# Scan outputs on TensorE: 64 output rows and 128 columns in two column groups instead of 32 rows and 64 columns in four

## The chip, the cores and the metric

The kernel runs on one core of a Trainium2 chip. The metric is device time in microseconds of one execution, smaller is better. Engines are named as in the profile: PE (TensorE matmuls), PEld (its weight loads), DVE (VectorE), ACT (ScalarE), POOL (GpSimd), SP (the engine that issues all DMAs here).

## The reference: what is computed

Sixteen images of 256 channels and 32 x 32 = 1024 positions go through two layers, each added to its input: group norm and a transformer block with four heads (attention over 1024 positions, then a feed-forward part), then group norm and a selective state-space layer. The second layer holds the recurrence that fills most of the time:

```python
def step(h, inp):
    d_t, B_t, C_t, u_t = inp
    dA = jnp.exp(d_t[..., None] * A)
    h = dA * h + (d_t * u_t)[..., None] * B_t[:, None, :]
    y = jnp.einsum('bdn,bn->bd', h, C_t)
    return (h, y)
h0 = jnp.zeros((B, D_INNER, D_STATE), u.dtype)
_, ys = lax.scan(step, h0, (delta..., Bm..., Cm..., u...))
```

D_INNER is 512, D_STATE is 64, and the scan runs over 1024 time steps. So an image has 512 x 64 recurrences of 1024 steps, and for every channel and time step a sum over 64 states of h times C. Everything is float32.

## The kernel before

**Units.** The recurrences of an image (a batch, in the code) are cut into 256 units. A unit is two channels of 64 states each, on 128 partitions, and all 1024 steps. With 16 batches there are 4096 units. For unit n the kernel does:

- `load`: a DMA brings the row of delta u of the two channels, repeated over 64 partitions each, into a tile `dub` (L928, 512 KB).
- `inputs`: POOL multiplies the tile by B in place (L933). B of the batch is in the tile `bt`.
- `decay`: PE spreads delta over the partitions by two bf16 products into a PSUM tile `a` of 1024 columns (L942), and ACT takes the exponential in place (L944). The pool `aps` has two such tiles.
- `scan`: DVE runs the recurrence over 1024 steps (L950) and writes row i of a buffer `h` of eight units.

**Products by C.** When eight units are done, `outputs` sums over the states. PE sums over partitions, but C changes with every time step. So the tile `cd` holds, for each time step, the 64 values of C in a column of their own (two columns, one for each channel of a unit; `spread_c` fills it from the tile `ct`). A product takes 16 columns of `cd` that are not zero, those of 8 time steps, in a block of 32, and h of the 8 units at the same 8 time steps: 64 columns. Of the 32 x 64 results only those where both time steps agree are wanted. Two such products (c = 0 and 1) fill disjoint rows of the 32 and are added in PSUM. Four groups g go to PSUM partitions 0, 32, 64 and 96, so to four column groups of PE. A float32 product is two instructions (records) in the trace, so the 128 products of eight units are 256 records, in eight steps of 32 records, one at each of the next eight units. The sums `yb[:, :256]` are copied to `y2` by ACT (L981) after every second step, four times in eight units.

**The turn.** After that, products of `y2` by `turn`, pieces of the unit matrix (L987), pick the wanted results and put the time steps on partitions: 32 products, 64 records, in one burst for every eight units. The weights that PE loads for them are columns of `y2` that stand eight elements apart. ACT copies the result to `yo` (L991), and two DMAs write it out.

**What else runs.** While batch b is scanned, the attention layer and the inputs of batch b + 1 and the last part of batch b - 1 are worked off in small steps (Python generators that yield shares of time; `rate` spreads them over the 256 units). The last batch has only the closing part of the one before it beside it. The steps that matter below are the scores (`s_ps`, L449), the weights and values (`st_ps` L520, `av` L508), the projections and the gate (L657, L679, L707).

**Order.** The order of instructions on PE, ACT, DVE and POOL is as written: in each unit `load(n + 6)`, `inputs(n + 4)`, one step of `outputs`, `scan(n)`, `decay(n + 2)`, then side steps. `decay(n + 2)` writes the PSUM tile that `scan(n)` reads. SP's order is left to a scheduler. All waits are semaphores which the framework places.

Of the kernel before, what the change touches and what calls it, by code (L numbers as in the profile page):

```python
# [11 lines left out]
F32 = mybir.dt.float32  # L12
# [7 lines left out]
P = 128  # L20
C = 256
KC = C // P
L = 1024
# [27 lines left out]
def attention_then_scan_kernel(  # L51
# [18 lines left out]
    nc = tc.nc  # L70
    B = x.shape[0]

    def pool(name, bufs, **kw):
        return ctx.enter_context(tc.tile_pool(name=name, bufs=bufs, **kw))

    const = pool("const", 1)
# [2 lines left out]
    half = pool("half", 4)  # L79
    ptp = pool("ptp", 4)  # L80
    small = pool("small", 2)
    dutp = pool("dutp", 7)
    blk = pool("blk", 2)
    hst = pool("hst", 1)
    dram = pool("dram", 2, space=DRAM)
# [44 lines left out]
    def hs(h):  # L130
        return ts(h, HL)
# [15 lines left out]
    ident = const.tile([P, P], F32, name="ident")  # L147
# [21 lines left out]
    for k in range(ND):  # L169
# [4 lines left out]
        for j in range(2):  # L174
# [3 lines left out]
                start=(j == 0), stop=(j == 1),  # L178
# [3 lines left out]
    for e in range(2):  # L182
        some = ident[ds(64 * e, 48), ds(64 * e, 48)].rearrange("p (r j i) -> p r i j", r=3, j=2)
# [8 lines left out]
        nc.vector.tensor_reduce(par[:, j : j + 1], ident[:, j:P:2], AX.X, ALU.add)  # L192


    turn = const.tile([P, 8, 2, 8], F32, name="turn")
    grid = ident.rearrange("p (m x j) -> p x j m", x=8, j=2)
    for c in range(8):
        nc.vector.tensor_copy(turn[:, c], grid[:, c])


# [22 lines left out]
    yb = yps.tile([P, HL], F32, name="yb", tag="yb")  # L223
    nc.vector.memset(yb, 0.0)

    cd = hst.tile([P, L // 16, 64], F32, name="cd", tag="cd")
# [129 lines left out]
    def fetches(to, src, n=KC):  # L356
        return [partial(fetch, to, src, k) for k in range(n)]


    def first_norm(b, besides=()):  # L360
        xs, tok = [], []
        kept = state[b]["kept"] = dram.tile([C, L], F32, name="kept", tag="kept")
        if "x" in state[b]:
            xs = state[b].pop("x")
        else:
            for go in fetches(xs, x[b]):
                go()
            yield 0.4
        gn = [work("gn") for _ in range(KC)]
        yield from along(group_norm(xs, gn), fetches(tok, pos) + [None] * 3 + list(besides))  # L370
        for k in range(KC):
            nc.gpsimd.tensor_tensor(tok[k], tok[k], gn[k], ALU.add)
            nc.sync.dma_start(kept[ts(k, P), :], tok[k])
            yield 0.6
# [461 lines left out]
    def gate_loads(b):  # L836
        st = state[b]
        (wo_s,), bring = weights((w_o, ND))
        ys, us, zs, gs, xs = [], [], [], [], []
        come = [  # L840
            partial(fetch, to, st[name], d)
            for d in range(ND) for to, name in ((ys, "ys"), (us, "ud"), (zs, "zs"))
        ]
        come.insert(1, bring[0])
        come += [
            partial(fetch, to, st[name], k) for k in range(KC) for to, name in ((gs, "gs"), (xs, "xr"))
        ]
        st["gate"] = ys, us, zs, gs, xs, wo_s, come[4:]
        return come[:4]

    def gate_and_store(b):
# [51 lines left out]
    units = [  # L903
        (b, k, q, e, i)
        for b in range(B) for k in range(ND) for q in range(4) for e in range(2) for i in range(SLOTS)
    ]
    blocks, loaded, decays = {}, {}, {}
    now = {}

    def load(n):  # L910
        b, k, q, e, i = units[n]
        st = state[b]
        if (k, q, e, i) == (0, 0, 0, 0):
            bt = hst.tile([P, L], F32, name="bt", tag="bt")
            ct = hst.tile([P, L], F32, name="ct", tag="ct")
            for v, lo in ((bt, 0), (ct, NS)):
                src = st["rows"][lo : lo + NS, :]
                nc.sync.dma_start(v, src.unsqueeze(1).to_broadcast([NS, 2, L]))
            blocks[b] = {"bt": bt, "ct": ct}
        if i == 0:  # L920
            pieces = blk.tile([P, HL], BF16, name="pieces", tag="pieces")
            rows = ds(((k * 4 + q) * 2 + e) * 48, 48)
            for hf in range(2):
                nc.sync.dma_start(pieces[ds(64 * hf, 48)], st["dps"][rows, hs(hf)])
            blocks[b, k, q, e] = pieces
        du = dutp.tile([P, L], F32, name="dub", tag="dub")
        src = st["dus"][ts(k, P)].rearrange("(q j i e) c -> q e i j c", q=4, j=2, i=SLOTS)[q, e, i]
        nc.sync.dma_start(du, src.unsqueeze(0).to_broadcast([NS, 2, L]))  # L928
        loaded[n] = du

    def inputs(n):
        v = loaded[n]
        nc.gpsimd.tensor_tensor(v, v, blocks[units[n][0]]["bt"], ALU.mult)  # L933
# [20 lines left out]


    def spread_c(b, c):
        ct = blocks[b]["ct"].rearrange("p (a c x) -> p a c x", c=2, x=8)
        for j in range(2):
            nc.scalar.activation(
                cd[:, :, 48 * c + j : 48 * c + j + 15 : 2], ct[:, :, c],  # L960
                AF.Identity, scale=par[:, j : j + 1],
            )

# [2 lines left out]

    def outputs(b, k, q, e):
        hbuf = now["h", e]
        y2 = hst.tile([P, 4, 256], F32, name="y2", tag="y2")
        for r in range(4):  # L970
            for s in range(4):
                for c in range(2):
                    for g in range(4):
                        at = 256 * r + 64 * s + 16 * g + 8 * c
                        nc.tensor.matmul(  # L975
                            yb[ts(g, 32), ts(s, 64)],
                            cd[:, at // 16, ts(c, 32)], hbuf[:, :, at : at + 8],
                            start=(c == 0), stop=(c == 1),
                        )
                if s == 3:  # L980
                    nc.scalar.copy(y2[:, r], yb[:, :256])  # L981
                if s % 2 == 1:
                    yield
        some = yb[:, 256:384].rearrange("p (j m x) -> p x j m", j=2, m=8)
        for x in range(8):
            for r in range(4):
                nc.tensor.matmul(  # L987
                    some[ts(r, 32), x], y2[:, r, x:256:8], turn[:, x], start=True, stop=True
                )
        yo = blk.tile([P, P], F32, name="yo", tag="yo")  # L990
        nc.scalar.copy(yo, yb[:, 256:384])  # L991
        for _ in range(3):
            yield
        to = state[b]["ys"][ds(k * P + 32 * q, 32)].rearrange(
            "(j i e) (a c) -> e j a i c", j=2, e=2, a=16
        )
        for j in range(2):
            nc.sync.dma_start(to[e, j], yo[:, ts(j, 64)])

    def prepare(b):  # L1000
        return chain(first_norm(b), attention_layer(b), scan_inputs(b))
# [6 lines left out]
    def gap(share, rate):  # L1008
        return share if share < 1 else max(1.0, share / rate)

    def rate_for(shares, room):
        lo, hi = 0.01, 10.0
        for _ in range(40):
            mid = (lo + hi) / 2
            lo, hi = (mid, hi) if sum(gap(w, mid) for w in shares) > room else (lo, mid)
        return hi
# [10 lines left out]
    running = []  # L1027
    side, rate, due = iter(()), 1.0, 0.0
    for n, (b, k, q, e, i) in enumerate(units):
        at = n % UNITS  # L1030
        if at == 0:
            parts = [prepare(b + 1)] if b + 1 < B else []
            total = steps * len(parts)
            if b > 0:
                if b + 1 < B:
                    parts = [
                        first_norm(b + 1, gate_loads(b - 1)), gate_and_store(b - 1),
                        attention_layer(b + 1), scan_inputs(b + 1),
                    ]
                else:  # L1040
                    parts = [gate_and_store(b - 1)]
                total = total + GATE
            side = chain(*parts)
            rate, due = rate_for(total, UNITS - AHEAD - 3), 0.0
        if at == UNITS - AHEAD:
            for _ in side:
                pass
            if b + 2 < B:
                for go in fetches(state[b + 2].setdefault("x", []), x[b + 2]):
                    go()  # L1050
        if n + AHEAD < len(units):
            load(n + AHEAD)
        if n + LEAD < len(units):
            inputs(n + LEAD)
        if n % UNITS == SLOTS:
            spread_c(b, 1)
        if i == 0 and n > 0:
            running.insert(0, outputs(*units[n - 1][:4]))
        for g in list(running):
            if next(g, g) is g:  # L1060
                running.remove(g)
        if n % UNITS == SLOTS - 1:
            spread_c(b, 0)
        scan(n)
        if n + 2 < len(units):
            decay(n + 2)
        if at >= (1 if b + 1 < B else 8):
            due -= 1.0
            while due <= 0.0:
                due += gap(next(side, 1e9), rate)  # L1070
# [76 lines left out]
```

## Time and profile before

| what | value |
|---|---|
| median of 3 runs | 12746.27 us (12697.65 to 12832.91) |
| profiled execution, its own time | 12803.03 us |
| span of the profiled execution | 12801.3 us |
| PE busy, PEld busy | 9998.7 us (78%), 5523.7 us (43%) |
| DVE busy | 11287.1 us (88%) |
| POOL busy | 10025.9 us (78%) |
| ACT busy | 7502.7 us (59%) |
| mean granted TensorE clock | 0.792 |

The busy time of an engine is the union of its instructions. PE's instructions are pipelined, so its busy time is not its full use. The line `PEclk` gives the clock that PE was granted in each fortieth of the span, in tenths of full speed. A view by windows gives the same numbers for chosen stretches of time. The view of the chain follows the work that ended last back from the end, piece by piece; a piece such as `PE yb L975 x32` is the time that these 32 records added to it.

### The profile page before, as it was taken

How to read it: one execution, taken by the hardware profiler on the slowest of the kernel's cores; microseconds unless marked ns; L12 is line 12 of the kernel's file. 1: busy time of each engine (PE TensorE's matmuls, PEld its weight loads, DVE VectorE, ACT ScalarE, POOL GpSimd, SP SyncE). 2: the span in 40 equal slices, each digit the busy share in tenths (PEclk: the TensorE clock that was granted, in tenths of full speed). 3: DMA queues.
4: the chain of work that ended last, by engine and by line, in shares of the span. 5: the costliest groups of instructions: out<-in, count | busy, mean ns of one | idle time of the engine just before them, and what ended most of it. 6: DMA issues, size and time to landing. Idle time of an engine off the chain costs nothing.

```text
span 12801.3 us, 424578 instructions
## 1 busy us (share of the span) xinstructions
PE 9998.7 (78%) x186800; PEld 5523.7 (43%) x186800; DVE 11287.1 (88%) x7480; ACT 7502.7 (59%) x10726; POOL 10025.9 (78%) x4201
## 2 busy tenths in 40 slices
PE   7776878868788786986978868787786877868777
PEld 2344444444444444443444444444444444444444
DVE  2799998989989899798798989989998999989998
ACT  3565665656566565565565656565565655656554
POOL 0587878878788788687778878787787878878798
PEclk8887978879788787686778878798787988879756
DMA  1567666676666767466566676666767667676676
GB/s 54 185 225 246 214 223 239 213 246 217 223 237 218 239 221 244 163 216 231 180 224 236 218 245 217 228 232 219 237 222 241 217 214 237 222 244 213 230 251 229
DMA packets 1038404, 2820.12 MB, mean 220 GB/s; under 512 B 290370, under 2 KB 368451, under 8 KB 1036548
## 3 DMA queue, kind: packets, MB, share of 16 engines
q1 hardware_dynamic: 1036548, 2792.97, 64.1%
q8 instruction: 1459, 23.90, 0.7%
q14 instruction: 397, 3.25, 0.1%
HBM read 2513.82 MB, written 261.62 MB: 217 GB/s over the span
## 4 chain that ended last, share of the span: by engine, by line
PE 41%; DVE 30%; issue 12%; ACT 8%; DMA 6%; POOL 2%; SPq 1%; DVEq 0%; POOLq 0%; ACTq 0%
DVE h L950 23%; PE s_ps L449 8%; PE yb L975 8%; PE a L942 6%; ACT a L944 4%; DMA dub<-dus 3%; PE av L508 3%; PE st_ps L520 3%; POOL dub L933 2%; PE z_ps L657 2%; PE yb L987 2%; PE g_ps L707 2%; PE m_ps L887 1%; DVE u L693 1%; DMA xs<-ud 1%
## 5 line engine op out<-in xcount | busy, mean ns | idle before, releaser
L933 POOL TENSOR_TENSOR dub<-dub,bt 128x1024 f32<-128x1024 f32 x4096 | 9800.5, 2416 | 2644.6 <-DMA dub<-dus 2458.8
L950 DVE TENSOR_TENSOR_SCAN h<-a,dub 128x1024 f32<-128x1024 f32 x4096 | 9204.1, 2276 | 708.7 <-ACT a L944 401.3
L944 ACT ACTIVATE a<-a,acol 128x1024 f32<-128x1024 f32 x4096 | 4464.2, 1090 | 3086.7 <-PE a L942 2954.9
L975 PEld LDWEIGHTS yb<-h,cd 128*32 128x32 f32 x131072 | 2517.7, 129 | 2704.1 <-issue 1303.3
L942 PE MATMUL a<-pieces,pick 48*128 48x512 bf16 x8192 | 1922.7, 460 | 2204.2 <-DVE h L950 2088.4
L975 PE MATMUL yb<-h,cd 128*32 128x64 f32 x131072 | 3292.0, 253 | 336.3 <-ACT y L981 231.8
L942 PEld LDWEIGHTS <-pick 48*128 48x128 bf16 x8192 | 571.7, 95 | 2612.3 <-issue 2204.8
L981 ACT COPY y<-yb 128x256 f32<-128x256 f32 x2048 | 763.3, 373 | 753.0 <-PE yb L975 744.2
L449 PE MATMUL s_ps<-kd,q 32*64 32x512 f32 x2044 | 593.4, 669 | 18.0 <-DVE mx L428 9.0
L508 PE MATMUL av<-pt,vv 128*64 128x512 f32 x2048 | 602.0, 668 | 2.8 <-ACT sums L497 1.6
L528 ACT ACTIVATE pt<-st_ps 128x512 f32<-128x512 f32 x1024 | 552.7, 597 | 73.5 <-PE st_ps L520 72.7
L987 PE MATMUL yb<-turn,y 128*32 128x16 f32 x32768 | 591.1, 214 | 4.9 <-issue 3.8
L520 PE MATMUL st_ps<-sp 33*128 33x512 f32 x2048 | 581.3, 643 | 3.4 <-ACT pt L528 3.4
L987 PEld LDWEIGHTS yb<-turn,y 128*32 128x32 f32 x32768 | 573.2, 159 | 5.8 <-issue 4.3
L449 PE MATMUL s_ps<-k,q 32*64 32x512 f32 x2048 | 569.1, 645 | 0.0
L428 DVE CUSTOM_DVE_ANT_0 over<-s_ps,over 128x512 f32<-128x512 f32 x512 | 343.8, 673 | 207.9 <-issue 120.6
L991 ACT COPY yo<-yb 128x128 f32<-128x128 f32 x512 | 135.3, 264 | 601.0 <-PE yb L987 581.3
L707 PE MATMUL g_ps<-w,xp 128*128 128x256 f32 x1464 | 455.2, 450 | 0.0
L707 PEld LDWEIGHTS g_ps<-w,xp 128*128 128x128 f32 x1464 | 367.9, 326 | 66.7 <-issue 58.5
L454 ACT ACTIVATE over<-s_ps 128x512 f32<-128x512 f32 x511 | 303.5, 594 | 86.7 <-PE s_ps L449 86.7
L887 PE MATMUL m_ps<-w,xs 128*128 128x256 f32 x1024 | 319.5, 462 | 11.5 <-POOL xs L862 11.5
L693 DVE SCALAR_TENSOR_TENSOR u<-up,cwh,u 128x1024 f32<-128x1024 f32 x192 | 301.7, 1571 | 28.0 <-ACT u L685 27.7
(178 smaller groups left out, 7103.6 us busy)
## 6 DMA issues: line engine op xcount, KB each, us to landing
dub<-dus SPq DMA_DIRECT2D x4096, 512.0 KB
dps<-pc SPq DMA_DIRECT2D x384, 128.0 KB
pieces<-dps SPq DMA_DIRECT2D x1024, 48.0 KB
xs<-in_x_dram SPq DMA_DIRECT2D x64, 512.0 KB
xs<-kept SPq DMA_DIRECT2D x64, 512.0 KB
zs<-z SPq DMA_DIRECT2D x64, 512.0 KB
ud<-u SPq DMA_DIRECT2D x64, 512.0 KB
dus<-du SPq DMA_DIRECT2D x64, 512.0 KB
```

Source lines behind the costliest of these rows:

```text
L449: nc.tensor.matmul(s[ts(e, 64)], q4[r, ts(c, 64)], keys[r], start=True, stop=True)
L508: nc.tensor.matmul(av[ts(e, 2 * DH)], vv[j // (NJ // 2)][:, j % (NJ // 2), 2 * pair + e, :], pts[e], start=(j == 0), stop=(j == NJ - 1),)
L520: nc.tensor.matmul(s, ka[r, ts(j, P)], qa[r, hs(hf)], start=True, stop=True)
L528: nc.scalar.activation(pt, s, AF.Exp)
L707: nc.tensor.matmul(ps[:, ts(q, C)], xp[k][:, ds(first + t, P, 4)], wg_s[:, k, t, :], start=(k == 0 and t == 0), stop=False,)
L933: nc.gpsimd.tensor_tensor(v, v, blocks[units[n][0]]["bt"], ALU.mult)
L942: nc.tensor.matmul(a[:, hs(hf)], w, pieces[r], start=True, stop=True)
L944: nc.scalar.activation(a, a, AF.Exp, scale=acol[:, at : at + 1])
L950: nc.vector.tensor_tensor_scan(now["h", e][:, i, :], decays.pop(n), loaded.pop(n), 0.0, ALU.mult, ALU.add)
L975: nc.tensor.matmul(yb[ts(g, 32), ts(s, 64)], cd[:, at // 16, ts(c, 32)], hbuf[:, :, at : at + 8], start=(c == 0), stop=(c == 1),)
L981: nc.scalar.copy(y2[:, r], yb[:, :256])
L987: nc.tensor.matmul(some[ts(r, 32), x], y2[:, r, x:256:8], turn[:, x], start=True, stop=True)
```

## The change

A product now takes the 32 columns of `cd` of 16 time steps in a block of 64, and h of eight units at 16 time steps: 128 columns. Two groups g go to PSUM partitions 0 and 64. So eight units have 64 products (128 records) in eight steps of 16 records. Each step fills 256 columns of `yb`, and each step is followed by a copy to `y2`, which has 8 x 256 columns instead of 4 x 256: eight copies in eight units. The first step of a new group of eight units is put before the turn of the group before it, and its copy after it. The turn has 16 x 2 products, each with a weight block of 64 columns of `y2`, 16 elements apart, and 8 columns of `turn`. The tiles `bt` and `ct` are taken from the pool of `dub`, which has 8 buffers instead of 7, so that B and C of the next batch no longer have one fixed buffer each. In the order that the program is built in, the loads of delta u wait for the scan seven units back, as before, except for some of them around the start of a batch, which wait for the one six or five units back.

```diff
-    dutp = pool("dutp", 7)
+    dutp = pool("dutp", 8)
...
-    turn = const.tile([P, 8, 2, 8], F32, name="turn")
-    grid = ident.rearrange("p (m x j) -> p x j m", x=8, j=2)
-    for c in range(8):
+    turn = const.tile([P, 16, 2, 4], F32, name="turn")
+    grid = ident.rearrange("p (m x j) -> p x j m", x=16, j=2)
+    for c in range(16):
...
-            bt = hst.tile([P, L], F32, name="bt", tag="bt")
-            ct = hst.tile([P, L], F32, name="ct", tag="ct")
+            bt = dutp.tile([P, L], F32, name="bt", tag="dub")
+            ct = dutp.tile([P, L], F32, name="ct", tag="dub")
...
-        ct = blocks[b]["ct"].rearrange("p (a c x) -> p a c x", c=2, x=8)
+        ct = blocks[b]["ct"].rearrange("p (a c x) -> p a c x", c=2, x=16)
+        to = cd.rearrange("p (a c) w -> p a c w", c=2)
...
-                cd[:, :, 48 * c + j : 48 * c + j + 15 : 2], ct[:, :, c],
+                to[:, :, c, 32 * c + j : 32 * c + j + 31 : 2], ct[:, :, c],
...
-        y2 = hst.tile([P, 4, 256], F32, name="y2", tag="y2")
-        for r in range(4):
-            for s in range(4):
+        y2 = hst.tile([P, 8, 256], F32, name="y2", tag="y2")
+        for u in range(8):
+            for s in range(2):
                 for c in range(2):
-                    for g in range(4):
-                        at = 256 * r + 64 * s + 16 * g + 8 * c
+                    for g in range(2):
+                        at = 128 * u + 64 * s + 32 * g + 16 * c
                         nc.tensor.matmul(
-                            yb[ts(g, 32), ts(s, 64)],
-                            cd[:, at // 16, ts(c, 32)], hbuf[:, :, at : at + 8],
+                            yb[ts(g, 64), ts(s, 128)],
+                            cd[:, at // 16], hbuf[:, :, at : at + 16],
                             start=(c == 0), stop=(c == 1),
                         )
-                if s == 3:
-                    nc.scalar.copy(y2[:, r], yb[:, :256])
-                if s % 2 == 1:
-                    yield
-        some = yb[:, 256:384].rearrange("p (j m x) -> p x j m", j=2, m=8)
-        for x in range(8):
-            for r in range(4):
+            if u == 0:
+                yield
+            nc.scalar.copy(y2[:, u], yb[:, :256])
+            yield
+        some = yb[:, 256:384].rearrange("p (j m x) -> p x j m", j=2, m=4)
+        sums = y2.rearrange("p (h u) w -> p h (u w)", h=2)
+        for x in range(16):
+            for h in range(2):
                 nc.tensor.matmul(
-                    some[ts(r, 32), x], y2[:, r, x:256:8], turn[:, x], start=True, stop=True
+                    some[ts(h, 64), x], sums[:, h, x:1024:16], turn[:, x], start=True, stop=True
                 )
...
-        if i == 0 and n > 0:
-            running.insert(0, outputs(*units[n - 1][:4]))
-        for g in list(running):
+        fresh = [outputs(*units[n - 1][:4])] if i == 0 and n > 0 else []
+        for g in fresh:
+            next(g)
+        for g in running + fresh:
             if next(g, g) is g:
                 running.remove(g)
+        running += fresh
```

## The prediction

> **What bounds the kernel now.** I read the page first: shares, slices, chain, groups.
>
> ```profile
> span 12801.3 us, 424578 instructions
> PE 9998.7 (78%) x186800; PEld 5523.7 (43%) x186800; DVE 11287.1 (88%) x7480; ACT 7502.7 (59%) x10726; POOL 10025.9 (78%) x4201
> PEclk8887978879788787686778878798787988879756
> PE 41%; DVE 30%; issue 12%; ACT 8%; DMA 6%; POOL 2%; SPq 1%; DVEq 0%; POOLq 0%; ACTq 0%
> L950 DVE TENSOR_TENSOR_SCAN h<-a,dub 128x1024 f32<-128x1024 f32 x4096 | 9204.1, 2276 | 708.7 <-ACT a L944 401.3
> L975 PE MATMUL yb<-h,cd 128*32 128x64 f32 x131072 | 3292.0, 253 | 336.3 <-ACT y L981 231.8
> L987 PEld LDWEIGHTS yb<-turn,y 128*32 128x32 f32 x32768 | 573.2, 159 | 5.8 <-issue 4.3
> ```
>
> DVE is nearly full, yet PE holds more of the chain: the bound changes by stage. So I asked for windows over batch 9 (in order: score stage, values, light stage, gate), the score stage of batch 7 (second row), and batch 15 (last):
>
> ```profile
> 7665.30:7734.60 69.30, 69.30 (x1202) 28.44 (x1203) 67.40 (x73) 42.75 (x64) 56.57 (x25) 1.00 0.55 192
> 6062.40:6189.10 126.70, 126.70 (x1202) 43.98 (x1200) 69.92 (x73) 45.74 (x64) 56.19 (x24) 0.50 0.31 105
> 7758.90:7883.60 124.70, 112.72 (x2248) 53.42 (x2249) 107.41 (x50) 96.52 (x148) 110.52 (x48) 0.93 0.67 231
> 7902.30:8031.40 129.10, 91.04 (x1746) 51.04 (x1745) 120.20 (x80) 68.40 (x91) 100.48 (x42) 0.72 0.62 214
> 8031.40:8128.80 97.40, 89.01 (x1496) 57.13 (x1495) 94.70 (x58) 58.28 (x80) 88.34 (x32) 0.96 0.68 225
> 12348.00:12716.40 368.40, 271.32 (x6760) 185.16 (x6760) 359.30 (x170) 205.11 (x261) 368.40 (x161) 0.60 0.71 242
> ```
>
> Columns: length, busy time of PE, PEld, DVE, ACT, POOL, then granted clock. The score stage is all PE; the same 24 units take 69.3 us at clock 1.00 and 126.7 at 0.50 (batches 6 and 7 of this execution; the others are at 1.00). Values and gate are near PE's limit (90%, 91%), the light stage is DVE's (93%), batch 15 POOL's (100%). The chain in the two score stages gives a unit piece by piece:
>
> ```profile
> 7687.48 0.58 PE yb L975 x32
> 7690.84 0.96 PE yb L987 x64
> 6057.65 3.61 PE s_ps L449 x8
> 6061.26 1.01 PE yb L975 x32
> 6089.01 0.54 PE a L942 x2
> ```
>
> At half clock 3.61 + 1.01 + 0.54 + 0.96/8 = 5.28 us a unit; at full clock (scores 1.86, decay 0.32 in the same view) 1.86 + 0.58 + 0.32 + 0.12 = 2.88.
>
> [...] L508 (64 columns, two groups) [...] in the trace its two records start 7 ns apart. [...] Here 110, 132 and 188 ns for 32, 64 and 128 columns side by side (L975, L508, L679): 0.81 ns a column over a base of 83. For strided columns [...] the trace has 160 ns for 32 (L987) and 329 for 128 (L707). [...] The trace has only 0.5 and 1.0, changing on multiples of 3.41 us; but a PE busy for 126.7 of 126.7 us stays at 0.50, so busy time is not the measure. [...]
>
> **What sets the clock.** I weighted each record by rows x columns of the array in use (a score record 32 x 64, so 1/8; four product records at once, all), times its streaming time at full clock, and summed over each clock window. Of half-clock windows under 0.25, none of 924 was followed by a full one; 0.30 to 0.35, 25% of 162; over 0.40, all 221. Of full-clock windows under 0.20 none of 143 stayed full; 0.25 to 0.30, 24% of 99; 0.30 to 0.35, 90% of 250. So a window needs use of about 0.3.
>
> **The change part by part.**
>
> Products. In the trace four records of 64 columns start 7 ns apart, the next four 55.8 ns later at full clock, 106.7 at half: time goes with columns and clock, not with records. L508's pairs of 512 columns stand 8 such steps apart. Two records of 128 columns should take two steps, 109 or 213 ns. A unit has 8 rounds before and after, so 8 x 53.4 = +0.43 us at full clock (0.58 to 1.01), +0.85 at half (1.01 to 1.86). Bounds: -0.1 (cost per record, half as many) to +0.9.
>
> The turn. Its 16 rounds of four take 62 ns each at both clocks, so matmul streaming isn't the limit. I take it to be the strided weight load: 62/32 = 1.94 ns a column; L707, one group of 128 strided columns, is spaced 233 ns, 1.8 a column[...]. So groups load side by side and the depth counts: 64 columns cost 124 ns, with two groups there are 32 rounds, 3.97 us for 0.96. Bounds: if it is writing 16 scattered columns to PSUM, 8 columns halve it (1.0 us in all); if a round is a fixed 62 ns, 2.0. I take 3.97: the weight loads are 50 ns longer than contiguous ones.
>
> Clock. The burst uses almost no array (8 columns a record), so a window half inside it falls to about 0.2: the clock drops at each burst. In the score stage at half clock a unit of 6.51 us would hold, as streaming time at full clock times share of the array: products 8 x 0.107 x 1, decay 0.21 x 0.75, four score pairs 4 x 0.427 x 0.25; in all 1.44, a use of 0.22. A window that holds a whole product block reaches 0.33. So the full clock seldom returns. I take one third full, two thirds half.
>
> Stage by stage, for 15 batches with work beside the scan:
> - Scores, 32 units. Full clock 1.86 + 1.01 + 0.32 + 3.97/8 = 3.69; half 3.61 + 1.86 + 0.54 + 0.50 = 6.51; mixed 5.57. 13 batches x 32 x (5.57 - 2.88) = 1119, two x 32 x 0.29 = 19. Together +1138.
> - Values, 50 units at 124.7/50 = 2.49. From the chain, a pair of L520 is 0.43, of L508 0.50; 1.25 and 1.125 pairs a unit: 1.10 + 1.01 + 0.32 + 0.50 = 2.93. So 0.44 x 50 x 15 = 330, and clock dips, 1.5 us at six bursts: 135. Together +465.
> - Gate, 33 units at 2.95: 1.56 of its own matmuls + 1.83 = 3.39, +218.
> - Light stages, 16 bursts. The product itself hides behind DVE. Not the burst, since `decay(n + 2)` stands behind it on PE, and behind that the exponential and the scan. From the end of scan n - 1 at half clock: decay 0.54, side work 0.3, products 1.86, burst 3.97, then ACT's yo copy 0.26, y2 copy 0.37 (now ahead of the exponential), exponential 1.09, hand-overs 0.15: 8.5 us, 7.5 at full clock (before: 4.3). DVE has two scans and three units' side work meanwhile, 3 x 3.0 - 2.28 = 6.7, or 8.1 where a unit takes 3.45. Late by 0 to 1.8; at 1.0, 16 x 15 = +240.
> - Batch 15, 32 bursts, 2 to 3 us late, partly recovered behind POOL: +80.
> - ACT's four more copies of 0.37 us in eight units: 0.19 a unit beside 41% idle time, counted only above. If values became ACT's, up to 0.1 x 50 x 15 = 75.
> - B and C. At the start of batch 8 the timeline has DVE waiting 6.51 us for POOL, and POOL for the delta u behind B. B's load now waits for a scan five units earlier: up to 6.5 x 15 = 98 gained. Loads with one or two units less lead are some 14 a batch, and cost nothing while POOL keeps four units of lead.
>
> Sum: 1138 + 465 + 218 + 240 + 80 - 98 = +2043 on the profiled 12803, so 14850. The profiled execution is 57 us above the median; one score stage at half clock costs 32 x 2.40 = 77, so runs differ by such stages. The forecast isn't moved by it, as all score stages end mixed.
>
> **Rivals.**
> A. The burst takes 2 us or less (PSUM writing or a fixed round). Scores +0.56 a unit at full clock, 233; values 142; gate 94; batch 15 20; B -98: 13200, up to 13700 with some clock dips. For it: the turn's outputs are scattered. Against: the long weight loads.
> B. The burst as forecast, but the clock holds in the score stage: scores +337 in place of 1138, without the values' dips 13910. For it: between bursts the use at full clock would be 1.44/3.19 = 0.45. Against: the window rule.
> C. Faster: cost by record, not by column. Products then stay at 0.58 or less and the burst at 0.96. Larger array use ends the half-clock score stages (-154) and B saves 98: 12550. It decides once a round of two wide records takes under about 65 ns. Against: the spacing doubles exactly with the clock, and L508.
>
> **Numbers.** Forecast 0.43; A 0.25; B 0.20; C 0.06; no change within 1%, if hidden costs and gains cancel, 0.04; above the range 0.02. About 1% is what can be told from no change here. The range 13150 to 15400 holds the forecast, A and B, with scores wholly at half clock (+500) at the top. Faster 0.06, same 0.04, slower 0.90.
>
> **What would show it.** A product piece of 16 records at 1.01 or 1.86 us; the turn's 64 records near 4 us and its weight loads near 210 ns; score windows of 24 units near 130 us with a clock between 0.5 and 0.8; DVE waiting for the exponential once in eight units; no 6.5 us wait at a batch's start. A turn under 2.2 us makes A right, a score clock above 0.9 B, product rounds under 65 ns C.

## The result and the profile after

The changed kernel takes 15685.15 us (median of 4 runs, 15678.48 to 15745.78). The kernel before takes 12777.05 us (median of 4). The ratio is 1.2326, with a 95% interval of 1.2275 to 1.2376: 23% slower. The forecast was 14850, with a range up to 15400. The direction and the main mechanisms were right, the size was not.

The page of the changed kernel, the lines that answer to those shown of before (span, busy times, clock by slices, chain, groups):

```profile
span 15688.6 us, 295315 instructions
PE 14172.0 (90%) x121264; PEld 8858.3 (56%) x121264; DVE 11442.4 (73%) x7488; ACT 8229.2 (52%) x12774; POOL 9950.9 (63%) x4201
PEclk8687786877878777787777877778687786877888
PE 69%; DVE 14%; ACT 7%; issue 6%; DMA 3%; SPq 0%; POOL 0%; DVEq 0%; POOLq 0%; ACTq 0%
L950 DVE TENSOR_TENSOR_SCAN h<-a,dub 128x1024 f32<-128x1024 f32 x4096 | 9252.8, 2280 | 2114.8 <-ACT a L944 1592.8
L976 PE MATMUL yb<-h,cd 128*64 128x128 f32 x65536 | 5688.8, 329 | 371.0 <-ACT y L983 248.6
L989 PEld LDWEIGHTS yb<-turn,y 128*64 128x64 f32 x32768 | 1864.0, 203 | 1.4 <-ACT y L983 1.4
```

PE now holds 69% of the chain, for 41% before. It has a third fewer records and is busy 4173 us longer. Its records overlap in the trace: 65536 of 329 ns in the mean stand in the 5688.8 us of L976's line. DVE does the same work (busy 11442.4 us for 11287.1) in a longer span. Its wait for the exponential ahead of the scan, the first releaser in L950's line, grew from 401.3 to 1592.8 us.

The windows over the same units as in the prediction (batch 9: scores, values, light stage, gate; batch 15 last; columns length, then busy PE, PEld, DVE, ACT, POOL, then clock):

```profile
9311.10:9462.10 151.00, 151.00 (x818) 68.12 (x816) 69.86 (x73) 49.64 (x76) 59.54 (x26) 0.53 0.26 92
9491.80:9647.00 155.20, 150.31 (x1478) 90.95 (x1478) 108.39 (x49) 104.84 (x173) 113.42 (x49) 0.89 0.51 184
9671.60:9810.90 139.30, 122.46 (x1106) 80.02 (x1105) 121.41 (x81) 74.63 (x111) 99.53 (x42) 0.80 0.59 200
9810.90:9933.70 122.80, 118.59 (x984) 80.73 (x983) 100.83 (x57) 63.37 (x96) 80.15 (x32) 0.92 0.52 174
15172.10:15592.50 420.40, 358.92 (x4200) 276.37 (x4199) 360.98 (x169) 232.48 (x341) 372.52 (x161) 0.83 0.61 211
```

The score stage went from 69.3 to 151.0 us for its 24 units, and its clock from 1.00 to 0.53. PE is busy in all of it. The other stages lose less, and their clocks change less, except in batch 15. There the clock rises from 0.60 to 0.83, and in the light stage from 0.72 to 0.80.

The chain in that score stage gives a unit's pieces:

```profile
9404.59 3.61 PE s_ps L449 x8
9408.20 1.91 PE yb L976 x16
9410.11 0.54 PE a L942 x2
9416.16 3.41 PE yb L989 x60
```

3.61 + 1.91 + 0.54 + 3.4/8 = 6.48 us. From the starts of the scans the trace has, in the mean over the batches, 6.48 us for units 50 to 57 and 6.3 for units 58 to 73. The prediction had 6.51 for the half clock.

Over all batches, from the starts of the scans in each trace, by stage (15 batches; units 0 to 39, 136 to 175 and 208 to 255 light, 40 to 79 scores and what ends them, 80 to 135 values, 176 to 207 gate):

| stage | before | after | difference | forecast |
|---|---|---|---|---|
| scores | 1887 | 3189 | +1302 | +1138 |
| values | 2134 | 2703 | +569 | +465 |
| gate | 1519 | 1848 | +328 | +218 |
| light, with the batch starts | 6189 | 6785 | +596 | +142 |
| batch 15 | 607 | 691 | +85 | +80 |

### The profile page after: what moved, and what is told of

Its sections match the earlier page's. It is cut to its first block, busy times and chain, and to the rows that moved or that the text cites. A ratio compares the mean times of both kernels' runs of the same rounds, so it can differ in the third digit from the quotient of the medians.

```text
span 15688.6 us, 295315 instructions
## 1 busy us (share of the span) xinstructions
PE 14172.0 (90%) x121264; PEld 8858.3 (56%) x121264; DVE 11442.4 (73%) x7488; ACT 8229.2 (52%) x12774; POOL 9950.9 (63%) x4201
## 4 chain that ended last, share of the span: by engine, by line
PE 69%; DVE 14%; ACT 7%; issue 6%; DMA 3%; SPq 0%; POOL 0%; DVEq 0%; POOLq 0%; ACTq 0%
PE yb L976 22%; PE s_ps L449 10%; PE yb L989 10%; DVE h L950 10%; PE a L942 6%; PE av L508 4%; PE st_ps L520 3%; ACT a L944 3%; PE g_ps L707 2%; PE m_ps L887 2%; PE z_ps L657 2%; ACT y L983 2%; DMA dub<-dus 1%; PE u_ps L679 1%; DMA xs<-ud 1%
## 5 line engine op out<-in xcount | busy, mean ns | idle before, releaser
L950 DVE TENSOR_TENSOR_SCAN h<-a,dub 128x1024 f32<-128x1024 f32 x4096 | 9252.8, 2280 | 2114.8 <-ACT a L944 1592.8
L976 PEld LDWEIGHTS yb<-h,cd 128*64 128x64 f32 x65536 | 4561.8, 167 | 2883.6 <-ACT y L983 917.4
L976 PE MATMUL yb<-h,cd 128*64 128x128 f32 x65536 | 5688.8, 329 | 371.0 <-ACT y L983 248.6
L983 ACT COPY y<-yb 128x256 f32<-128x256 f32 x4096 | 1530.1, 374 | 3205.0 <-PE yb L976 3187.5
L989 PEld LDWEIGHTS yb<-turn,y 128*64 128x64 f32 x32768 | 1864.0, 203 | 1.4 <-ACT y L983 1.4
L989 PE MATMUL yb<-turn,y 128*64 128x8 f32 x32768 | 1848.4, 253 | 0.9 <-ACT y L983 0.9
L942 PEld LDWEIGHTS <-pick 48*128 48x128 bf16 x8192 | 479.0, 95 | 1734.7 <-issue 1681.5
L449 PE MATMUL s_ps<-kd,q 32*64 32x512 f32 x2044 | 869.4, 953 | 18.1 <-DVE kd L423 9.1
L449 PE MATMUL s_ps<-k,q 32*64 32x512 f32 x2048 | 848.9, 932 | 0.0
L508 PE MATMUL av<-pt,vv 128*64 128x512 f32 x2048 | 640.0, 707 | 2.9 <-ACT sums L497 1.6
L449 PEld LDWEIGHTS s_ps<-k,q 32*64 32x64 f32 x2048 | 208.7, 199 | 535.4 <-issue 504.8
```

What stands on the lines that cost most here:

```text
L449: nc.tensor.matmul(s[ts(e, 64)], q4[r, ts(c, 64)], keys[r], start=True, stop=True)
L508: nc.tensor.matmul(av[ts(e, 2 * DH)], vv[j // (NJ // 2)][:, j % (NJ // 2), 2 * pair + e, :], pts[e], start=(j == 0), stop=(j == NJ - 1),)
L942: nc.tensor.matmul(a[:, hs(hf)], w, pieces[r], start=True, stop=True)
L950: nc.vector.tensor_tensor_scan(now["h", e][:, i, :], decays.pop(n), loaded.pop(n), 0.0, ALU.mult, ALU.add)
L976: nc.tensor.matmul(yb[ts(g, 64), ts(s, 128)], cd[:, at // 16], hbuf[:, :, at : at + 16], start=(c == 0), stop=(c == 1),)
L983: nc.scalar.copy(y2[:, u], yb[:, :256])
```

## The experiments

**Parts of the change taken out (e1, e2, e3).** First the turn, then half of the products, then both. e1 in the changed kernel:

```diff
-        for x in range(16):
+        for x in range(1):
             for h in range(2):
```

> The changed kernel with 1 of the turn's 16 column steps kept, so 15/16 of the turn is left out; products unchanged. Theory 1 (the burst of 3.6 us drops the clock in the score stage and stands ahead of the decay elsewhere): score stage back to clock above 0.9 and near 3.2 us a unit (1.86 + 1.01 + 0.32), for 6.48; light stages nearly as in the kernel before; in all about 13100. Theory 2 (the light stages lose by the wider products, since side matmuls queue behind them): scores as in theory 1, but light stages keep most of their +600; about 13500. Rival (the clock falls because of the wider products, not because of the burst): the score stage stays at 0.5 and near 6.0 us a unit, 14400.

e2 in the changed kernel:

```diff
-                for c in range(2):
+                for c in range(1):
...
-                            start=(c == 0), stop=(c == 1),
+                            start=True, stop=True,
```

> The changed kernel without the products of c = 1: half of the products are left out, so that a unit has 8 records of 128 columns and products take 0.58 or 1.01 us as before; the turn is whole. Theory 1: scores stay at half clock, 3.61 + 1.01 + 0.54 + 0.45 = 5.6 us a unit; values and gate each get 0.43 us a unit back; light stages stay slow; about 14700. Theory 2: light stages lose most of their +600 as well, 14200. Rival (products set the clock): score stage at full clock, 3.2 us a unit, below 13500.

e3 has both edits.

> Both of the last two left out: half of the products and 15/16 of the turn. What remains of the change is the double number of copies, their place ahead of the exponential, and B and C from the other pool. All theories with PE as the cause: score stage 2.77 us a unit at full clock in all batches, in all 12500 (between 12350 and 12650). Rival (ACT's copies, or the loads with less lead, cost time by themselves): above 12800.

Measured: e1 13040.37, e2 15008.71, e3 12651.67 us (one run each; the kernel before took 12682.1 on that chip). The window rows of e1's and e2's score stage in batch 9, in this order, columns as above:

```profile
7753.10:7830.50 77.40, 77.40 (x638) 34.87 (x636) 69.67 (x73) 46.59 (x76) 56.41 (x25) 1.00 0.53 172
8911.60:9043.10 131.50, 131.50 (x626) 48.17 (x624) 69.81 (x75) 49.41 (x76) 60.49 (x26) 0.53 0.32 105
```

Without the burst the clock stays at 1.00 although the products are wide; with it the clock is 0.53 although the products are halved. So in this stage the burst decides the clock, and the rival of e1 and e2 falls. 77.4/24 = 3.2 us a unit is 1.86 + 1.01 + 0.32 of the expectation.

The three spans and the changed kernel's make a table of two by two: neither part 12650, wide products alone 13039 (+389), burst alone 15007 (+2357), both 15689 (+3039, which is 293 more than the sum). The burst is the main cost by a factor of six. The remaining parts (more copies, their place, B and C's pool) cost little: e3 is not above the kernel before, though it is just above the range expected for it. It also lacks the short turn that the kernel before has, so a small cost of these parts may be hidden by that.

In the light stages the same table reads: neither 6170, products 6325 (+155), burst 6540 (+370), both 6785 (+615). So theory 2, products as the main cause there, is wrong; theory 1, products quite hidden, is not exact either. e2 came out above both expectations: values 471 and light stages 351 above before, each more than I had for a burst beside narrow products.

**The burst alone, in the kernel before (e4).**

```diff
-        for x in range(8):
+        for x in [x for x in range(8) for _ in range(4)]:
             for r in range(4):
```

> The kernel before with each matmul of the turn issued four times (same result): a burst of about 3.84 us in place of 0.96, products unchanged. Theory 1: the clock falls to half in all score stages, 3.61 + 1.01 + 0.54 + 0.48 = 5.6 us a unit; light stages late by the burst; about 14500. Theory 2: the same scores, light stages little changed, 14100. Rival (a burst on its own does not drop the clock): score stage at 1.0 and 3.25 us a unit, below 13500.

Measured: 16473.84 us, above every expectation. The burst is not 3.84 us. Its median from first to last record is 6.83 us, since PE stands still in it without a wait that the profile shows:

```profile
L987 PE MATMUL yb<-turn,y 128*32 128x16 f32 x131072 | 2299.1, 217 | 1374.0 <-issue 1372.5
```

1372.5 us of idle time by "issue" in 512 bursts is 2.7 us a burst. The clock of the score stages was 0.57 to 0.69, for 0.94 to 1.00 in 13 of the 15 before, so this burst beside narrow products did lower it. For the sizes the run says nothing, since it was not the burst that was meant. What holds PE up in a run of 256 records was not tried.

**Why the burst takes its time (e5b).** The copies write `y2` in another order, so that each weight load reads 64 neighbours:

```diff
-        y2 = hst.tile([P, 8, 256], F32, name="y2", tag="y2")
+        y2 = hst.tile([P, 2, 16, 64], F32, name="y2", tag="y2")
...
-            nc.scalar.copy(y2[:, u], yb[:, :256])
+            nc.scalar.copy(
+                y2[:, u // 4, :, ts(u % 4, 16)], yb[:, :256].rearrange("p (m x) -> p x m", x=16)
+            )
...
-                    some[ts(h, 64), x], sums[:, h, x:1024:16], turn[:, x], start=True, stop=True
+                    some[ts(h, 64), x], y2[:, h, x], turn[:, x], start=True, stop=True
```

> The changed kernel, but ACT's copies write y2 in the order in which the turn loads it, so that the 64 columns of each weight load lie side by side (same result). Theory (the burst's 3.34 us are the strided weight loads): load time down from 203 ns to about 132, as L508's, and the burst to 32 x 53 ns = 1.7 us; the clock still drops in part of the score stages; between 13300 and 14500. Rival (the burst's time is a fixed cost of a round or of scattered PSUM writing): burst stays at 3.3 us and the time at 15690.

Measured: 14437.21 us (one run), 1250 below the changed kernel. The weight loads in a light window of the changed order, from the view of one line (min, median, max in ns):

```profile
L990 PEld LDWEIGHTS yb<-turn,y x314: 137/138/138, 7999.9 to 8091.2; 128*64 128x64 f32 x157
```

The load fell from 203 to 138 ns, and the burst at full clock from 3.34 to 1.79 us (medians from the first to the last record's start). The output's scattered columns are unchanged, so at full clock they are not what made the burst 3.34 us long: the strided loads are. The page's group of the copies has 374 ns in both orders. The score stage is the interesting rest: its mean clock is 0.5 to 0.59 in 11 batches and 1.0 in 4. What decides between the two with this burst was not tried. The 24 units of batch 9 take 155.2 us at 0.50. Of the 1397 us that e5b's span lies above e1's, the scores hold 1114 (2982 for 1868).

**A burst of the same length on the whole array (e6b).** 15/16 of the turn are left out; in their place:

```diff
+        other = now["h", 1 - e]
+        for _ in range(4):
+            for s in range(2):
+                for c in range(2):
+                    for g in range(2):
...
+                            yb[ts(g, 64), ts(s, 128)],
+                            cd[:, at // 16], other[:, :, at : at + 16],
...
```

> As e1 (15/16 of the turn left out), and in the turn's place the products of the burst's own unit are issued four times again: 64 records as in the turn, 4 x 0.87 = 3.5 us at full clock, but on the whole array. Theory (low use during the burst is what drops the clock): the score stage stays at clock 1.0, (3.19 + 3.5/8) = 3.63 us a unit, 1740 for its 480 units in place of 2751; other stages lose as by any burst; about 14000. Rival (any burst of this length delays the decays and so brings the half clock, whatever it computes): score stage near 6 us a unit, 15500 or more.

Measured: 14391.12 us (one run), some 390 above the expectation. This burst takes 3.42 us (median), for 3.34 of the turn. The score stage of batch 9:

```profile
8539.60:8627.60 88.00, 88.00 (x830) 45.05 (x828) 69.64 (x73) 46.58 (x76) 56.09 (x24) 1.00 0.45 151
```

88.0/24 = 3.67 us a unit at clock 1.00, as expected (3.63). The mean clock of the stage is between 0.85 and 1.0 in all batches. Five of the stages began at half clock, and all five went back to full clock at their first dense burst. In the changed kernel 14 stages began at full clock, and all fell to half at their first burst beside the scores. All 40 score units of 15 batches take 2260 us, for 1868 in e1 and 3189 with the turn. The one burst takes 3.42 us and the other 3.34, so it was what the burst computes that set the clock here, not its length: the rival falls. The two runs also split the burst's cost: e6b is 1351 us above e1, which is delay; the changed kernel is 1299 us above e6b, which is the clock, 929 of it in the scores. The split is rough: the two bursts are not equally long, and the half-clock starts of e6b's five stages count as delay here (seven units each at 6.05 in place of 3.2 us, about 100 us by this estimate).

**B and C's pool, and contiguous weights, in the kernel before (e7b, e8b).** e7b has only the change's three lines on `dutp`, `bt` and `ct`.

> The kernel before with one part of the change: tiles of B and C from the pool of delta u's tiles, with 8 buffers. Theory: the wait of 6.5 us at the start of 15 batches shrinks; 0.4 to 0.8% faster (50 to 98 us). Rival (loads with one or two units less lead, and loads that stand in line behind those of B and C, take it back): no change.

Ratio 0.9983 (0.9956 to 1.0009): no difference that can be told. From the scans' starts, the last eight units of a batch take 2.4 us each instead of 3.0, so most of the wait at the start of a batch is gone (some 5 us). But units 8 to 15 take 4.4 instead of 4.1, which gives some 2.3 us back. Why was not tried. All light stages together are 23 us shorter.

e8b adds the order of e5b to the four-group turn:

```diff
-        y2 = hst.tile([P, 4, 256], F32, name="y2", tag="y2")
+        y2 = hst.tile([P, 4, 8, 32], F32, name="y2", tag="y2")
...
-                    nc.scalar.copy(y2[:, r], yb[:, :256])
+                    nc.scalar.copy(y2[:, r], yb[:, :256].rearrange("p (m x) -> p x m", x=8))
...
-                    some[ts(r, 32), x], y2[:, r, x:256:8], turn[:, x], start=True, stop=True
+                    some[ts(r, 32), x], y2[:, r, x], turn[:, x], start=True, stop=True
```

> The kernel before with that part and with the turn's weights contiguous as in e5b (same result). Theory: the burst falls from 0.93 to about 0.5 us; that is 0.05 us a unit in the score stage (25 us) and little elsewhere, so with B and C about 1% faster (80 to 130 us). Rival: the burst is off the path and nothing more than in e7b is gained.

Ratio 0.9894 (0.9866 to 0.9922), 1.1% faster than before. The burst fell from 0.93 to 0.55 us at full clock. Its single runs go from 12492 to 12771 us: in the profiled one, the slowest of them, three score stages were at half clock.

**Scores that use more of the array (e9).** In e8b, the loop over head pairs goes inside the loop over keys:

```diff
-            for g in range(2):
-                maxima()
-                pair = []
-                for keys in (kd, k4[:, hs(1)]):
-                    s = psum3("s_ps")
+            overs = []
+            for keys in (kd, k4[:, hs(1)]):
+                maxima()
+                pair = [psum3("s_ps") for g in range(2)]
+                for g in range(2):
                     for e in range(2):
                         r = ts(2 * g + e, DH)
...
```

> As e8b, and the score products of both head pairs are issued together, so that four products of 32 rows and 64 columns stand in four row groups and two column groups (same result). Theory (the clock goes by use of the array, and score records at half clock make PE the bound): score matmuls take about 0.95 us a unit at full clock and 1.8 at half, so a unit at half clock is 1.8 + 1.0 + 0.54 + 0.07 = 3.4 us instead of 5.2; use at half clock rises to 1.03/3.4 = 0.30, near the bound, so half-clock score stages get rare and cheap; at full clock DVE's 2.8 us is the bound. 12450 to 12550, 1.2 to 2% below the kernel before, with a smaller spread of runs. Rival (four row groups don't run at once, or waits for three PSUM tiles eat it): as e8b or slower.

Measured: 12527.01 us (12512.41 to 12548.85), ratio to before 0.9864 (0.9812 to 0.9916). The score stage of batch 9, same 24 units:

```profile
7457.60:7524.60 67.00, 52.51 (x1204) 25.02 (x1200) 67.00 (x73) 43.41 (x64) 56.43 (x25) 1.00 0.62 199
```

PE is busy 52.5 of 67.0 us and DVE all of it: the bound has moved. In the profiled execution all 15 score stages are at clock 1.0, or 0.94 in the first, and the four runs spread over 36 us instead of 139 us (seven runs of the kernel before, beside it). By the median e9 is 57 us below e8b, whose best runs are as fast. So what it takes away seems to be the half-clock score stages; this rests on one trace and four runs. It is faster than both kernels.

## Why the prediction was wrong, step by step

**Products: right.** 0.58 became 1.02 us at full clock, 1.01 became 1.91 at half; forecast 1.01 and 1.86. A unit has 16 records of 128 columns for 32 of 64. From one round of two to the next it is 109 ns at full clock and 213 at half in the trace of after, for 55.8 and 106.7 from one round of four to the next before. So the time went with columns, not with records, and rival C falls. One reading behind the forecast was loose: L508's pairs stand 480 ns apart at full clock in the trace of before, which is 8.6 steps and not 8.

**The burst: right in cause, 19% too long.** Forecast 3.97 us, measured 3.34; the load 203 ns for some 210. The depth of the strided columns counts (203 ns for 64, 160 for 32), and e5b shows that the stride is what costs (138 ns for 64 side by side). Rival A falls. That scattered columns of the output slow a burst was a guess of mine which no view of before showed.

**The clock: right in cause, wrong in "one third full, two thirds half".** In 14 of the 15 batches the score stage (units 42 to 73) begins at full clock, falls to half at its first burst, that of unit 49, and does not return; in batch 0 it is at half from the start. So a quarter of the units, not a third, comes before the fall. Units 42 to 49 take 3.9 us in the mean, 50 to 57 6.48 and 58 to 73 6.3: 5.76 over all 32, for my 5.57. For the full share I had counted on windows that reach a use of 0.33. A window is 3.41 us: the clock records of both traces (620 before, 1140 after) change between 0.5 and 1.0 on multiples of 3.413 us only. Weighted in the same way, they are there in the changed kernel: about 170 of some 600 clock windows in these half-clock stages have a use of 0.30 to 0.35. But none of the 170 was followed by a full one. Over its whole trace 2% of some 500 half-clock windows with that use were, for 25% before. So the table of clock windows held in direction: none of some 600 windows under 0.25 was followed by a full one and all of some 470 over 0.40 were, and the dense burst of e6b kept the clock where the sparse one lost it (1.00 and 0.53 in batch 9). Its bound of about 0.3 did not carry over to the wide products. Why is open.

The half-clock unit, 6.48 us for 6.51, is so close in part by luck: the products took 0.05 more and the burst 0.08 less. The stage's miss of 164 us has two halves: units 42 to 73 rose by 1216 us for my 1138, and another 85 us lie in units 40 and 41, where a burst stands just ahead of the scores and which my 32 units left out. Rival B falls: it needs a score clock above 0.9, and batch 9 has 0.53.

**The light stages: the failed step.** The forecast was 240, less 98 for B and C; measured +596, the largest miss (454 of 837 us in the table). Three terms were wrong. First, "The product itself hides behind DVE": by e1 against e3 it costs 155 us. Second, "late by 0 to 1.8; at 1.0": by e2 against e3 the burst costs 370/240 = 1.5 us each time although it was shorter than forecast, and with wide products 90 us more in all, 460 for 240. Third, B and C gained about nothing (e7b; the light stages of e3 are 19 us below those of before, for a forecast of 98).

What ended DVE's idle time before its scans shows where the first two come from. Two waits in one light stage of the changed kernel, from the timeline (start, length, instruction, then idle time before it and what ended that):

```profile
8062.75 4.47 DVE L950 TENSOR_TENSOR_SCAN h<-a,dub 128x1024 f32<-128x1024 f32 x2 [1.39 <-PE yb L976]
8070.53 2.29 DVE L950 TENSOR_TENSOR_SCAN h<-a,dub 128x1024 f32<-128x1024 f32 x1 [1.99 <-ACT a L944]
```

The first scan is that of the first unit of a group of eight. It writes into a buffer `h` that the last products of the group two back still read, and it waits for them. In all light stages such waits are 57 us in e3 and 189 in e1. That is 132 of the product's 155 us, and a wait that my sum did not have. The second scan is that of the third unit, whose decay stands right behind the burst: the path that I had followed. Its waits for the exponential are 24 us in e3 and 309 in e2, 38 in e1 and 350 in the changed kernel. So this path costs 285 beside narrow products and 312 beside wide ones, for my 240. The other 85 and 148 us of the burst came another way. The chain through the same burst shows it:

```profile
8060.69 1.91 PE yb L976 x16
8065.42 3.45 PE yb L989 x64
8069.05 0.39 ACT y L983
8069.48 1.21 PE yb L976 x16
8070.69 0.56 PE a L942 x2
8071.28 1.09 ACT a L944
8072.36 0.54 ACT sp_s L785
8072.91 0.56 ACT d_ps L786
8073.49 0.71 DVE d_ps L790
8074.83 0.58 DVE h L950
```

The chain goes one unit further: the copy after the burst frees `yb`, the next unit's product waits for that copy, and its decay for the product. Then the exponential stands ahead of side work on ACT, that side work ahead of side work on DVE (L790), and this ahead of the scan. A late PE reaches the scan through the side work's queues as well, not only through its own decay. DVE's waits for ACT ahead of L790 grow by 55 us from e3 to e2 and by 81 from e1 to the changed kernel; the rest of this way was not separated.

**Values and gate: too small by 104 and 110.** The sums 2.93 and 3.39 us a unit supposed full clock and added 1.5 us for each dip in the values, nothing in the gate. e1 is 60 and 62 us above the kernel before, for the products, and e6b against e1 gives 330 and 196 us for a burst with little loss of clock. That makes 390 and 258, for my 330 and 218. The clock then adds 179 and 71; forecast for values' dips was 135, for the gate's none.

**Batch 15** (+85 for +80) was right, and e1 (608) and e2 (686) put it down to the burst.

## What to carry to other kernels

Before a tile shape on PE is changed, list every product that follows from it, weight loads included: here the product that was meant was not the expensive one, but the turn behind it, whose strided loads doubled in depth and in rounds (a burst of 3.34 us for 0.93). Look at what a burst does to the stages that are PE-bound, and at their clock, however busy PE is: with a burst of 8-column records the score stage of batch 9 had a clock of 0.53, with one of 128-column records 1.00, and PE was busy all the time in both. And when work is put in front of an engine's queue, follow the delay through each buffer that is freed late, the one that a longer product still reads as well as the one that the next unit waits for.

## What the runs showed of the hardware

- The granted clock did not go by busy time. Bursts of 3.34 us (64 records of 8 columns) and of 3.42 us (64 records of 128 columns) in the same place gave 0.53 and 1.00 in the score stage of batch 9. PE was busy all the time in both. What fits is the share of the array in use over the windows of 3.41 us between which the clock changes in both traces, weighted as in the prediction: in the changed kernel none of some 600 windows under 0.25 was followed by a full one, and all of some 470 over 0.40 were. There is no one bound: with a use of 0.30 to 0.35, 25% of 162 half-clock windows of the kernel before were followed by a full one, and 2% of some 500 in the changed kernel.
- The turn's strided weight loads took the same time at either clock: 203 ns in the changed kernel and 160 before, at full as at half clock (contiguous ones of L975: 110 and 177). The burst of 64 records takes 3.34 us at full and 3.36 at half clock. With contiguous loads (e5b) it does go by the clock: 1.79 and 3.28 us. So at half clock the better order gains 0.08 us a burst, for 1.55 at full clock.
- The same order change, on four column groups of 32 (e8b), gives 0.55 us at full and 0.84 at half clock, for 0.93 and 0.95 before.
- A run of 256 matmul records in one burst (e4) had 2.7 us of idle issue time in the mean, where the kernel before's bursts of 64 had next to none (3.8 us in 512).
